# A graph network of four layers on one core: buffer order, division order and a transfer route changed together

## The chip, the cores and the metric

The kernel runs on one core of a Trainium2 chip. A core has TensorE (matrix products, PE in the profile; its loads of weights are PEld), VectorE (DVE), ScalarE (ACT), GpSimd (POOL) and SyncE (SP). SP, GpSimd and ScalarE also issue transfers (DMA), which sixteen DMA engines carry out. Each engine works through its own queue in order and waits on semaphores. The metric is the device time of one execution in microseconds (us); lower is better. Before the change the median of three runs is 3392.79 us (3391.16 to 3394.97).

## The reference

The input is a matrix `x` of 3327 nodes by 512 features and a sparse 0/1 adjacency `adj` of 3327 by 3327. Four layers follow each other, and each is `x = layernorm(x + layer(x, adj))`.

Layers 0, 2 and 3 are graph attention. For layer 3, cut to what matters:

```
h = (x @ W).reshape(N, 4, 128).transpose(1, 0, 2)        # a projection, 4 heads
e = leaky_relu(si[:, :, None] + sj[:, None, :], 0.2)     # si, sj: h times the two halves of a
e = where(adj > 0, e, -9e15)
h_prime = softmax(e, axis=-1) @ h                        # a sum over neighbours, per head
return elu(h_prime)                                      # heads side by side: N x 512
```

Layers 0 and 2 have eight heads of 64 features; layer 0 has no `elu`. Layer 1 takes the mean over the first 64 neighbours of each node, projects it and the node itself, and adds the two.

## The kernel before, in words

The nodes are cut into `NT` = 26 row tiles of 128. All intermediate tensors between the stages lie in DRAM: `hd` holds the sums of an attention over the neighbours before they are divided by the denominators, `rec` (on chip) the reciprocals of these denominators, and `x2`, `x3` the results of the layers, which are the residuals of the next.

**Attention** (`unit`, from line 364). An attention layer runs over two halves of the result's rows (13 tiles, 1664 nodes) and, within a half, over four slots `s`: two heads of 64 in layers 0 and 2, one head of 128 in layer 3. A unit is one (half, slot). Over the 26 tiles `j` of source nodes, VectorE makes the unnormalised weights `t` (line 405), ScalarE makes a mask `y` of the larger branch from them (line 408), and TensorE adds the products of `t` and the projected features `vj` into four PSUM banks `po` (line 428), and those of `y` into banks `pd` for the denominators (line 380). Three buffers of `t` let VectorE be ahead of TensorE. At the unit's end `po`, features by nodes, is copied to `ob` and has to be transposed. There are two ways:

- `by_dma`, in the first half of layer 3: VectorE transposes `po` in blocks of 32 by 32 into `ob` (line 446), and four transfers put the blocks at their places in `hd` (line 473).
- otherwise: VectorE copies the first bank (line 450) and ScalarE the other three (line 448), and during the following unit jobs of up to four TensorE transposes each (line 456) bring `ob` into `pt`. In layer 3's second half the function `final` takes `pt` from there: for heads 0 and 1 VectorE copies it into `g` (line 1010), a tile on chip with the second half's rows. The jobs `first_slots` later divide these columns of `g`, take the exponential and add the residual.

**The end of a layer** (`finish_steps`, lines 165 to 203). For `n` row tiles, `load` takes the sums `h` from `hd` and the residual `xr`; `divide` multiplies `h` by `rec` on VectorE (line 181) and, with `elu`, takes the exponential on ScalarE (line 186); `add` adds the residual (lines 194 and 195, or 197); `norm_rows` computes mean and variance (152, 153), the root (154), the reciprocal (155), a product (158) and scales on ScalarE (161). The tiles come from pools. A pool lays its tiles in memory in the order in which their names first appear, each with its number of buffers. A pool may lie over memory of pools closed before; its tile then waits for the last use of the older tiles that it lies over. So the order of names sets what a load waits for.

The function is used at the end of layers 0 and 2 for the first two tiles, in `sage` (layer 1, pool `sa`: six `h` of 2 KB, then two `xr`), in `third` (the last projection, pool `p_f`: ten `h`, six `xr`) and in layer 3's second half for the rows of the first.

In layer 1's first stage (963 to 1168 us) tile after tile is normalised, transposed (line 724) and multiplied with two matrices (732, 735). The tiles of layer 0's end that its loads lie over are those of layer 0's last unit. In the memory plan the six `h` of `sa` begin at byte 188672 of a partition and the two `xr` are at 200960 and 203008. Layer 0 used 182656 to 189311 for its last buffer of `t`, 189312 to 200959 for seven `y`, 200960 to 205055 for `vj`, and 200960 for the last small `hb`, which is stored to `hd`.

**The last projection** (`third`, from line 892). For every tile the result of layer 2 is finished, stored, transposed by TensorE (261), copied by ScalarE (262, `xT`), summed by VectorE (263, `xsum`) and, one tile later, multiplied with the weights (271); ScalarE takes three small parts of the product (`dc`, `rc`, `qc`, lines 272 and 275) and VectorE scales the rest (277, `vt`). Two tiles make a group. The loop's order in the text is:

```
for s, y in enumerate(ys):
    xT = L3.project1(pp, ps, y, t)            # transposes, xT, xsum
    if s == 0 and groups:
        ahead, steps = groups.pop(0)
        for f in steps:                       # divide, add, norm_rows of the next group
            f()
    if pend:
        L3.project2(pp, bank, wsb, *pend)
```

After tile 14 `prepare` and `cut` are called for the first half, small operations that make the next attention's columns.

**What sets the order.** TensorE's instructions stay as written. On the other engines and queues a planner picks, at each step, the earliest written instruction that its own estimate of times holds to be ready. An instruction whose data the planner believes to be there early may so stand in the queue far ahead of its place in the text; on the chip the engine waits for it all the same. `tc.keep_in_program_order(ins)` puts `ins` behind the instruction that was written just before it for the same engine. Before the change this holds for the exponential of tile 2 (`pinned` with `t0 == 2`, `s == 0`).

Of the kernel before, what the change touches and what calls it, by code (L numbers as in the profile page):

```python
# [7 lines left out]
F32 = mybir.dt.float32  # L8
# [5 lines left out]
ALU = mybir.AluOpType  # L14
# [4 lines left out]
P = 128  # L19
# [13 lines left out]
def kernel(  # L33
# [10 lines left out]
    nc = tc.nc  # L44
    N, F = x.shape
# [66 lines left out]
    rec = const.tile([P, NT, 8], F32, name="rec")  # L112
# [52 lines left out]
    def finish_steps(pool, xin, layer, t0, n, hbufs=6, eng=nc.sync, xbufs=None, xpool=None, ebufs=None, pinned=False):  # L165
        H, D = layer.H, layer.D
        ys, xs, steps = [], [], []

        def load():
            for t in range(t0, t0 + n):  # L170
                h = pool.tile([P, F], F32, name="h", bufs=hbufs)
                load_tile(h, hd, t, eng)
                ys.append(h)
                xr = xpool.tile([P, F], F32, name="xr", tag="hb") if xpool else \
                    pool.tile([P, F], F32, name="xr", bufs=xbufs)
                load_tile(xr, xin, t, nc.gpsimd)
                xs.append(xr)

        def divide(s):
            h = ys[s]  # L180
            nc.vector.tensor_tensor(h.rearrange("p (h d) -> p h d", h=H), h.rearrange("p (h d) -> p h d", h=H),
                                    rec[:, t0 + s, :H].rearrange("p (h e) -> p h e", e=1).to_broadcast([P, H, D]),
                                    op=ALU.mult)
            if layer.elu:
                e = pool.tile([P, F], F32, name="e", bufs=ebufs)
                ins = nc.scalar.activation(e, h, AF.Exp)
                if pinned and s == 0:
                    tc.keep_in_program_order(ins)
                xs.append(e)

        def add(s):
            h, xr = ys[s], xs[s]
            if layer.elu:
                nc.vector.scalar_tensor_tensor(xr, xs[n + s], 1.0, xr, op0=ALU.min, op1=ALU.add)
                nc.vector.scalar_tensor_tensor(h, h, 0.0, xr, op0=ALU.max, op1=ALU.add)
            else:
                nc.vector.tensor_tensor(h, h, xr, op=ALU.add)

        steps.append(load)
        for s in range(n):  # L200
            steps += [lambda s=s: divide(s), lambda s=s: add(s)]
        steps.append(lambda: norm_rows(pool, ys, t0))
        return ys, steps

    def finish(*a):
        ys, steps = finish_steps(*a)
        for f in steps:
            f()
        return ys
# [16 lines left out]
    class Layer:  # L226
# [137 lines left out]
        def unit(self, pools, half, s, background, aside, final=None, ending=None):  # L364
            H, D, HS = self.H, self.D, self.HS
# [73 lines left out]
            den(NT - 2, late)  # L439

            ob = sp.tile([P, IW], F32, name="ob", bufs=1)
            by_dma = HS == 1 and not final
            for c, (a_, z) in enumerate(CUTS):
                if by_dma:

# [5 lines left out]
            t0 = half * HALF  # L451
# [16 lines left out]

            nothing = lambda: None
            jobs = [nothing, nothing]  # L470
            if by_dma:
                for b in range(4):
                    nc.sync.dma_start(out=hd[i0:i0 + IW, s * P + 32 * b:s * P + 32 * b + 32]
                                      .rearrange("(q i) f -> i q f", i=32),
                                      in_=ob[32 * b:32 * b + 32, :].rearrange("p (q f) -> p q f", f=32))
# [16 lines left out]
            if not by_pe:  # L492
# [3 lines left out]
                for c in range(2):  # L496
                    ins = nc.vector.transpose(db[:64, c * (WA // 2):(c + 1) * (WA // 2)], pd[c][:64, :WA // 2])
# [394 lines left out]
    def third(first):  # L892
        with tc.tile_pool(name="col3", bufs=1) as cp, tc.tile_pool(name="at_r3", bufs=2, reuse_waits="tile") as rp:
# [3 lines left out]
            with tc.tile_pool(name="p_w", bufs=1, reuse_waits="tile") as wp, \  # L897
# [13 lines left out]
                def load_group(t0):  # L911
                    if t0 < NT:
                        groups.append(finish_steps(fp, x2, L2, t0, 2, 10, nc.gpsimd if t0 < 4 else nc.sync, 6,
                                                    pinned=t0 == 2))
                        groups[-1][1].pop(0)()

                load_group(2)
# [3 lines left out]
                for t0 in range(0, NT, 2):  # L921
# [4 lines left out]
                    for s, y in enumerate(ys):  # L926
# [3 lines left out]
                        if s == 0 and groups:  # L930
                            ahead, steps = groups.pop(0)
# [14 lines left out]
            with tc.tile_pool(name="f3", bufs=2) as fp, tc.tile_pool(name="f4", bufs=1) as gp:  # L946
                g = gp.tile([P, HALF, F], F32, name="g")
# [57 lines left out]
                    return [divide, add]  # L1005

                def final(s, q0, n, pt):
                    qs = slice(q0, q0 + n)
                    if s < 2:
                        nc.vector.tensor_copy(g[:, qs, s * P:(s + 1) * P], pt[:, :n])  # L1010
                        return

                    y = g[:, qs, s * P:(s + 1) * P]
                    held = {}
# [210 lines left out]
```

## Time and profile before

| | us |
|---|---|
| median of three runs | 3392.79 |
| the profiled execution | 3389.15 |
| its span, first to last instruction | 3387.4 |
| busy in the span: PE, PEld | 3251.2, 1626.4 |
| busy in the span: DVE, ACT, POOL | 2687.5, 2354.6, 239.8 |

| stage | from and to, us | PE busy | DVE busy | ACT busy |
|---|---|---|---|---|
| layer 0, attention | 137 to 958 | 796.66 | 806.43 | 753.93 |
| layer 1, first stage | 958 to 1168 | 194.15 | 137.79 | 71.06 |
| layer 1, second stage | 1168 to 1755 | 572.32 | 252.15 | 199.82 |
| layer 2, attention | 1755 to 2553 | 781.78 | 791.54 | 738.53 |
| last projection | 2553 to 2690 | 119.16 | 110.95 | 100.14 |
| layer 3, first half | 2690 to 3020 | 328.85 | 211.53 | 177.66 |
| layer 3, second half and end | 3020 to 3387 | 341.80 | 294.74 | 285.71 |

The profile shows one execution. A line of a timeline gives start and duration in us, the engine (PE, PEld, DVE, ACT, POOL; SPq for the issue of a transfer by SP), the line of the kernel, the operation, output and inputs, the count, and in brackets how long the engine had stood idle before and what it waited for. A line of the chain (the work that ended last, followed back from the end) gives start, duration, engine, output and line. Times of TensorE are modelled from its pipelining, so that a busy TensorE need not be at its peak.

### The profile page before, as it was taken

What the parts mean: (1) busy time and instruction counts of PE and PEld (TensorE: products, weight loads), DVE (VectorE), ACT (ScalarE), POOL (GpSimd) and SP (SyncE); (2) the same over time, 40 slices, a digit from 0 to 9 for tenths busy, and PEclk for the clock granted to TensorE, in tenths of its full rate; (3) what the DMA queues carried; (4) which work ended last, traced back from release to release, by engine and by line L of the source; (5) the groups of instructions that cost most, each with busy time, mean ns of one, the idle gap of its engine ahead of it and who ended that gap; (6) DMA issues with size and microseconds to landing.
All of it is one profiled execution on the core that took longest, in us unless ns stands there. A gap on an engine that the chain in (4) does not pass through costs nothing.

```text
span 3387.4 us, 47182 instructions
## 1 busy us (share of the span) xinstructions
PE 3251.2 (96%) x18476; PEld 1626.4 (48%) x18476; DVE 2687.5 (79%) x2619; ACT 2354.6 (70%) x2143; POOL 239.8 (7%) x389
## 2 busy tenths in 40 slices
PE   8899999999979999999989999999998999999997
PEld 7634344444434445545544444444446754455453
DVE  5799999999967544444449999999998766668887
ACT  2398998999953333333338999999997655558986
POOL 3100000000010011111110000000002000010110
PEclk9999999999999999999999999999998999999998
DMA  9644111110143343333320111111117411122211
GB/s 368 222 124 127 49 49 38 55 49 28 44 123 125 122 117 84 91 85 87 80 77 20 47 48 50 51 48 47 35 31 241 152 41 42 41 51 80 94 42 49
DMA packets 288014, 284.29 MB, mean 84 GB/s; under 512 B 107492, under 2 KB 223534, under 8 KB 287791
## 3 DMA queue, kind: packets, MB, share of 16 engines
q1 hardware_dynamic: 254063, 170.62, 16.6%
q0 software_dynamic: 28208, 102.96, 9.5%
q10 hardware_dynamic: 5520, 7.69, 0.7%
q8 instruction: 146, 2.39, 0.3%
q14 instruction: 77, 0.63, 0.1%
HBM read 212.01 MB, written 69.17 MB: 83 GB/s over the span
## 4 chain that ended last, share of the span: by engine, by line
PE 85%; DVE 5%; DMA 4%; ACT 3%; issue 2%; SPq 0%; ACTq 0%; DVEq 0%; POOL 0%; POOLq 0%
PE po L428 52%; PE acc L859 12%; PE pd L380 7%; PE pw L271 5%; DVE t L405 3%; PE pz L732 3%; DMA raw<-in_adjT_dram 3%; PE pi L735 3%; ACT y L408 1%; PE pt L456 1%; PE pk L819 1%; DMA h<-hd 0%; PE pa L1108 0%; PE pt L724 0%; PE pct L664 0%
## 5 line engine op out<-in xcount | busy, mean ns | idle before, releaser
L405 DVE SCALAR_TENSOR_TENSOR t<-rb,qc,mask 128x1664 f32<-128x1664 f32 x1040 | 1960.3, 1954 | 169.4 <-PE po L428 147.3
L408 ACT ACTIVATE y<-t,bi,sc 128x1664 fp8e4<-128x1664 f32 x1040 | 1769.5, 1766 | 310.4 <-PE pd L380 292.7
L428 PE MATMUL po<-t,vj 128*64 128x448 f32 (+3 forms) x8320 | 1909.6, 521 | 22.1 <-DVE t L405 19.6
L428 PEld LDWEIGHTS po<-t,vj 128*64 128x64 f32 (+1 forms) x8320 | 838.9, 148 | 970.6 <-issue 704.0
L859 PE MATMUL acc<-zs,kt 128*128 128x512 bf16 x1352 | 401.1, 380 | 0.0
L271 PE MATMUL pw<-wsb,xT 128*128 128x264 f32 (+1 forms) x1248 | 302.2, 397 | 15.2 <-DVE vt L277 12.0
L859 PEld LDWEIGHTS <-kt 128*128 128x128 fp8e4 x2002 | 196.1, 98 | 242.1 <-issue 7.7
L811 ACT CAST pk<-cy 128x512 f32<-128x512 bf16 x169 | 99.0, 588 | 277.4 <-DVE kt L823 266.3
L271 PEld LDWEIGHTS pw<-wsb,xT 128*128 128x128 f32 x1248 | 241.1, 197 | 60.7 <-ACT xT L262 10.8
L380 PE MATMUL pd<-y,sden 128*32 128x448 fp8e4 (+1 forms) x4160 | 259.5, 342 | 10.4 <-ACT y L408 10.4
L859 PE MATMUL acc<-zl,kt 128*128 128x512 bf16 x650 | 246.5, 379 | 0.0
L380 PEld LDWEIGHTS <-sden 128*32 128x32 bf16 x4160 | 117.5, 96 | 162.5 <-issue 139.8
L823 DVE SCALAR_TENSOR_TENSOR kt<-pk,mask 128x512 fp8e4<-128x512 f32 x169 | 116.1, 688 | 94.0 <-PE pk L819 94.0
L277 DVE TENSOR_TENSOR vt<-pw,dc 128x256 f32<-128x256 f32 x156 | 59.0, 418 | 148.2 <-ACT dc L272 143.7
L359 POOL DMA_DIRECT2D rb<-r x40 | 21.3, 532 | 1670.4 <-DVE t L405 1652.2
L275 ACT COPY rc<-pw 128x8 f32<-128x8 f32 (+1 forms) x78 | 12.6, 162 | 156.6 <-PE pw L271 154.1
L831 DVE SCALAR_TENSOR_TENSOR y<-acc,cnt,bnb 128x512 f32<-128x512 f32 x26 | 19.5, 751 | 97.7 <-PE acc L859 90.3
L732 PE MATMUL pz<-wn,xT 128*128 128x512 f32 x208 | 94.9, 600 | 1.7 <-ACT xT L726 1.7
L700 POOL DMA_DIRECT2D cy<-ctd x91 | 67.9, 746 | 385.1 <-ACT pk L811 312.6
L735 PE MATMUL pi<-wl,xT 128*128 128x512 f32 x208 | 93.5, 592 | 0.0
L634 DVE TENSOR_SCALAR mask<-raw 128x832 fp8e4<-128x832 int32 (+2 forms) x90 | 54.8, 614 | 38.9 <-DMA raw<-in_adjT_dram 38.5
L154 ACT ACT_TABLE_LOAD x45 | 57.7, 1283 | 37.0 <-DVE mv L153 36.4
(187 smaller groups left out, 1699.3 us busy)
## 6 DMA issues: line engine op xcount, KB each, us to landing
vj<-v SPq DMA_DIRECT2D x312, 128.0 KB
rb<-r POOLq DMA_DIRECT2D x40, 832.0 KB, 4.8
raw<-in_adjT_dram SPq DMA_DIRECT2D x67, 416.0 KB
cy<-ctd POOLq DMA_DIRECT2D x78, 256.0 KB, 4.0
h<-hd SPq DMA_DIRECT2D x61, 256.0 KB
v<-vt SPq DMA_DIRECT2D x50, 256.0 KB
hd<-hb SPq DMA_DIRECT2D x48, 256.0 KB
xr<-x POOLq DMA_DIRECT2D x45, 256.0 KB, 3.1
```

The costliest lines, as they stand in the source:

```text
L271: nc.tensor.matmul(pw[e][:, :FW + H], xT[:, c, :], wsb[:, c, e, :], start=c == 0, stop=c == FC - 1)
L277: nc.vector.tensor_tensor(vt[:, hs, :], pw[e][:, :FW].rearrange("p (h d) -> p h d", d=D), self.dc[:, t, hs].rearrange("p (h e) -> p h e", e=1)
L380: nc.tensor.matmul(pd[c][32 * kk:32 * kk + 32, :w_], lhsT, rhs, start=(kk, c) not in seen, skip_group_check=final is not None, stop=last a ...
L405: nc.vector.scalar_tensor_tensor(t, rb[k], self.qc[:, j, h:h + 1], mask[:, j, i0:i0 + IW], op0=ALU.max, op1=ALU.mult)
L408: nc.scalar.activation(y, t, AF.Sigmoid, bias=self.bi[:, j, h:h + 1], scale=self.sc[:, j, h:h + 1], saturate=False)
L428: nc.tensor.matmul(po[c][k * D:(k + 1) * D, :z - a_], vj[:, j % 2, k * D:(k + 1) * D], ts[k][:, a_:z], start=j == 0, stop=j == NT - 1)
L700: nc.gpsimd.dma_start(out=cy[:, :n, :], in_=ctd[t:t + n, b * GW:(b + 1) * GW] .rearrange("(o t) i -> o t i", o=1).to_broadcast([P, n, GW]))
L732: nc.tensor.matmul(pz, xT[:, c, :], wn[:, c, :], start=c == 0, stop=c == FC - 1)
L735: nc.tensor.matmul(pi, xT[:, c, :], wl[:, c, :], start=c == 0, stop=c == FC - 1)
L811: nc.scalar.copy(pks[k % 2], carry[b, t // 4 * 4][:, t % 4:t % 4 + 2, :])
L823: nc.vector.scalar_tensor_tensor(kt, pk, NEIGHBOURS, mask[:, t:t + 2, i0:i0 + GW], op0=ALU.is_le, op1=ALU.mult, saturate=False)
L859: nc.tensor.matmul(acc, kts[t][:, s * P:(s + 1) * P], zs(t, c) if c < 2 else zl[:, t, :], start=t == 0 and c == 0, stop=t == NT - 1 and c ...
```

## The change

It has three parts.

1. In `finish_steps`, `load` asks for the tile `xr` before the tile `h`. The transfers keep their order. In a pool in which neither name has appeared before, the buffers of `xr` now come first.
2. In `third`, every group is `pinned`. For such a group both divisions are written before both additions, and from tile 4 on (`t0 > 2`) each division stays behind the VectorE instruction written before it: for the first of a group that is `xsum` of the first tile of the group before. The exponential of tile 2 is kept in order as before.
3. In the second half of layer 3, heads 0 and 1 take the route `by_dma`. VectorE transposes in blocks into `ob`, and sixteen transfers per head, issued on SP, bring the blocks from `ob` to their places in `g`, both on chip. The TensorE transposes and the copies by VectorE and ScalarE of these two heads are gone.

```diff
         def load():
             for t in range(t0, t0 + n):
+                xr = xpool.tile([P, F], F32, name="xr", tag="hb") if xpool else \
+                    pool.tile([P, F], F32, name="xr", bufs=xbufs)
                 h = pool.tile([P, F], F32, name="h", bufs=hbufs)
                 load_tile(h, hd, t, eng)
                 ys.append(h)
-                xr = xpool.tile([P, F], F32, name="xr", tag="hb") if xpool else \
-                    pool.tile([P, F], F32, name="xr", bufs=xbufs)
                 load_tile(xr, xin, t, nc.gpsimd)
...
         def divide(s):
             h = ys[s]
-            nc.vector.tensor_tensor(h.rearrange("p (h d) -> p h d", h=H), h.rearrange("p (h d) -> p h d", h=H),
+            ins = nc.vector.tensor_tensor(h.rearrange("p (h d) -> p h d", h=H), h.rearrange("p (h d) -> p h d", h=H),
...
+            if pinned and t0 > 2:
+                tc.keep_in_program_order(ins)
             if layer.elu:
                 e = pool.tile([P, F], F32, name="e", bufs=ebufs)
                 ins = nc.scalar.activation(e, h, AF.Exp)
-                if pinned and s == 0:
+                if pinned and (t0, s) == (2, 0):
                     tc.keep_in_program_order(ins)
...
         steps.append(load)
-        for s in range(n):
-            steps += [lambda s=s: divide(s), lambda s=s: add(s)]
+        if pinned:
+            steps += [lambda s=s: divide(s) for s in range(n)] + [lambda s=s: add(s) for s in range(n)]
+        else:
+            for s in range(n):
+                steps += [lambda s=s: divide(s), lambda s=s: add(s)]
...
-            by_dma = HS == 1 and not final
+            by_dma = HS == 1 and (not final or s < 2)
...
-            if by_dma:
+            if by_dma and final:
+                for b in range(4):
+                    for m in range(4):
+                        final(s, b, m, ob[32 * b:32 * b + 32, :].rearrange("p (q m f) -> p q m f", m=4, f=32)[:, :, m, :])
+            elif by_dma:
...
-                                                    pinned=t0 == 2))
+                                                    pinned=True))
...
                 def final(s, q0, n, pt):
+                    if s < 2:
+
+                        nc.sync.dma_start(out=g[32 * n:32 * n + 32, :, s * P + 32 * q0:s * P + 32 * q0 + 32], in_=pt)
+                        return
                     qs = slice(q0, q0 + n)
-                    if s < 2:
-                        nc.vector.tensor_copy(g[:, qs, s * P:(s + 1) * P], pt[:, :n])
-                        return
```

More of the change, by code (lines that the diff above doesn't have):

```diff
@@ L180, in divide @@
             h = ys[s]
-            nc.vector.tensor_tensor(h.rearrange("p (h d) -> p h d", h=H), h.rearrange("p (h d) -> p h d", h=H),
-                                    rec[:, t0 + s, :H].rearrange("p (h e) -> p h e", e=1).to_broadcast([P, H, D]),
-                                    op=ALU.mult)
+            ins = nc.vector.tensor_tensor(h.rearrange("p (h d) -> p h d", h=H), h.rearrange("p (h d) -> p h d", h=H),
+                                          rec[:, t0 + s, :H].rearrange("p (h e) -> p h e", e=1).to_broadcast([P, H, D]),
+                                          op=ALU.mult)
+            if pinned and t0 > 2:
+                tc.keep_in_program_order(ins)
             if layer.elu:
```

## The prediction

> **What bounds the kernel now.** I read the page first: TensorE is busy for 96% of the span and its lines hold 85% of the chain that ended last. So a stretch where TensorE is fed gains only what TensorE itself is spared, and the rest lies in its holes. I then went through the chain, the timeline of each engine and a table of stretches for the three places which the edits touch.
>
> Place 1, layer 0 to layer 1. In the timelines of GpSimd, VectorE and TensorE:
>
> ```profile
> 969.73 0.54 POOL L126 DMA_DIRECT2D xr<-in_x_dram  x1 [9.92 <-issue]
> ...
> 967.63 0.69 DVE L181 TENSOR_TENSOR h<-h,rec 128x512 f32<-128x512 f32 x1 [5.85 <-DMA h<-hd]
> 972.85 0.69 DVE L197 TENSOR_TENSOR h<-h,xr 128x512 f32<-128x512 f32 x1 [4.53 <-DMA xr<-in_x_dram]
> 977.21 0.69 DVE L181 TENSOR_TENSOR h<-h,rec 128x512 f32<-128x512 f32 x1 [2.25 <-DMA h<-hd]
> ...
> 983.97 1.11 PE L724 MATMUL pt<-ident,h 128*128 128x128 f32 x4 [13.84 <-ACT h L161]
> ```
>
> GpSimd stands for 9.92 us before it loads the residual of row tile 2; VectorE waits for that residual, and TensorE idles 13.84 us for the normalised tile. The memory plan says on what GpSimd waits: that buffer lies at byte 200960, over the last `hb` of layer 0, whose store leaves last.
>
> Place 2, the last projection, in the timelines of VectorE and TensorE and the table of stretches (us and count for PE, PEld, DVE, ACT, POOL, then clock, DMA share and GB/s):
>
> ```profile
> 2562.96 1.40 DVE L181 TENSOR_TENSOR h<-h,rec 128x512 f32<-128x512 f32 x2 [4.52 <-DMA h<-hd]
> ...
> 2573.51 1.12 PE L261 MATMUL pt<-ident,h 128*128 128x128 f32 x4 [8.46 <-ACT h L161]
> ...
> 2600.00:2620.00 20.00, 17.72 (x90) 15.05 (x89) 19.19 (x45) 13.80 (x36) 1.61 (x3) 1.00 0.75 251
> 2660.00:2680.00 20.00, 20.00 (x103) 17.37 (x103) 8.85 (x17) 8.68 (x25) 0.00 (x0) 1.00 0.25 96
> ```
>
> VectorE is stuck 4.52 us in a division for tile 4, whose sums are late, while the additions of tile 2, ready since the exponentials ended at 2560.62, queue behind it; TensorE idles 8.46 us. Later VectorE works far ahead (19.19 of 20) and ends early (8.85 of 20).
>
> Place 3, the last layer's second half. The chain at the start of head 1, then the one place that shows the new route, the end of the first half:
>
> ```profile
> 3115.28 0.44 PE pt L456 x4
> 3115.71 2.80 PE po L428 x8
> 3118.51 0.49 PE pd L380 x6
> ...
> 3018.86 2.10 DVE L446 STREAM_TRANSPOSE ob<-po 128x448 f32<-128x448 f32 x4
> ...
> 3020.99 4.46 SPq L473 DMA_DIRECT2D hd<-ob  x4
> ```
>
> TensorE's transposes of the previous head stand on the path, and the transposing by VectorE with four stores went by there without a hole.
>
> **What the Trainium skill says.** Perfetto Trace Analysis, Tensor Engine Instruction, calls VectorE and ScalarE strict FIFOs: the 4.52 us above are such a queue. ScalarE: Activation LUTs, What ACT_TABLE_LOAD costs, gives 1283 ns for a load plus 1380 ns of drain; the loads here last 1283 ns, but a root follows a load by 0.01 us (2585.83, 2587.12), so only 1.28 is priced. TensorE: Matmul & The Clock Gate, What's actually happening, lets the clock fall after about 3.4 us of idleness: after 8.46 us sixteen products took 5.42 instead of 3.67 us, after 1.30 us they took 3.75; the trace agrees. DMA: Bandwidth & Descriptors, Why small descriptors are slow, exempts transfers within SBUF; nothing before shows one of that kind.
>
> **Part 1: residual buffers first.** No instruction changes. In layer 1's pool two `xr` (4 KB) move ahead of six `h`, so tile 2's and 3's residuals land at 188672 and 190720, over `t` and `y`, which are free when the last `pd` products end at 958.28. GpSimd then issues the four loads of tiles 2 and 3 from 959.26 in a row, 0.54 each, to 961.4. The 0.75 MB more that now move share the engines with 0.96 MB of stores at some 340 GB/s, so they land by 970.4 (estimate). Then the add 0.7, statistics and aggregate 0.85, root 0.35, reciprocal and product 0.4, the first scaling 0.8 and handovers 0.15: the transposes start at 973.65 instead of 983.97, **-10.3**. From there TensorE is full (40.00 of 40 in three stretches from 1000), so it reaches the end. Late next is the load of `h` for tile 4, which now lies over that `hb` and stands behind six small loads on SP (landed 977.2): TensorE needs tile 4 at about 988. It costs nothing unless VectorE's queue again has tile 4's division ahead of tile 3's addition; then nearly all of the gain is gone (bounds -12 and -1). The other pools: in the last projection the two waits (1.20 and 1.09 us on GpSimd) only change hands, between `xr` and `h`; in the last layer `xr` had its place already. Zero, bounded by 1 us either way.
>
> **Part 2: divisions in written order.** Each group's first division from tile 4 on is queued behind `xsum` of the group before; no work comes or goes. First the gain: tile 2's additions follow the exponentials at once: four at 0.6 to 0.7 (2559.7 to 2562.3), statistics 1.4, one `xsum` 0.6, root, reciprocal and product 0.9, scaling 0.8: 2566.0 instead of 2573.51, **-7.5**.
>
> Then the loss: groups can no longer run ahead. One period, scaling to scaling: two scalings 1.5, copy of `xT` 0.59, `xsum` 0.60, first division 0.68, exponential 0.63, four additions 2.5, statistics 1.28, aggregate 0.17, root 0.29, reciprocal 0.16, product 0.16, and nine handovers of 0.05: 9.0 us. TensorE needs 7.9 for two tiles (0.44 + 3.51 each), so the chain bounds. VectorE has 2.1 us of other work per group (four `vt` at 0.37, one `xsum` at 0.6); I put half inside the chain: 10.1. The halves of `prepare` and `cut`, 5.4 us of VectorE once, find 2 us free per period: 3 us remain. Tiles 2 to 24 are eleven groups: 11 x 10.1 + 3 = 114.1 us; before, 2672.70 - 2573.51 = 99.2. **+14.9**. Bounds for the period: 9.0 with all else in gaps (99.0, so -0.2), 11.4 with a table load of 1.28 in every chain (128.4, so +29.2).
>
> **Part 3: two heads by transfer.** Removed: 26 transposes, in the chain 0.44 x 3 + 0.11 for head 0 and 0.59, 0.58, 0.59, 0.11 for head 1: 3.3 us of TensorE. ScalarE loses three copies a head (1.5 us), VectorE trades one copy (0.62) and four (2.34) for four transposes (2.1 to 2.3). SP gets 2 x 16 issues; 416 pieces of 128 bytes each are 6656 a head, as many as the four stores of one head before (4.46 us of issue; DMA busy until about 3029). Queued behind them on SP: `vj`, three pairs ahead (19 us), and a load of `h`, for which VectorE already waited 2.83 us at 3107.83. I charge 0.8 us for that and for VectorE's 1.7 us more at the turn into head 2. **-2.5**; bounds -3.5 and +3.
>
> **Sum.** -10.3 - 7.5 + 14.9 - 2.5 = -5.4 us on the profiled 3389.15 (span 3387.4 and 1.75 around it): 3383.7. The median of the runs is 3392.79, 3.64 higher, so 3387.4.
>
> **Rivals.** *Short chain*: the planner puts VectorE's other work into gaps, period 9.3, 1.5 for `prepare`: 103.8, so +4.6; sum -15.7, 3377. For it: VectorE loses its 6.1 us of waits for `h`, and has 2 us idle in each period. Against: a filler between reciprocal and product is common now (2587.45 to 2588.71).
> *Long chain, slower*: in the last projection each root is followed by an exponential set's load for `dc` before the scaling, as now at 2613.43 and 2631.26: period 11.4, 128.4 us, sum +8.9, 3402. The whole comes out at zero from a period of 10.6, and slower from 11.2.
> *Place 1 keeps its hole*, because tile 4's division blocks as at 977.21: gain 1 instead of 10.3, 3396.7. The change then does not do there what it says.
>
> **How the numbers follow.** Sum 0.35 (3382 to 3392 alone), short chain 0.30, long chain 0.18, hole kept 0.17. About 0.2%, 6.8 us, can be told from no change: 3386.0 to 3399.6. Faster: 0.14 of the first and nearly all of the second, 0.42. Same: 0.21, 0.015, 0.02 and 0.14, 0.39. Slower: 0.19. The range takes the second and third cases in: 3372 to 3404.
>
> **What would show it.** Right: GpSimd's residual load near 960, TensorE's hole at 970 down to 4 us; no wait of L181 for DMA near 2560; the transposes of L261 in pairs every 10 us with 1 to 2 us idle; L456 26 fewer, no new hole near 3107 and 3191. Wrong: the hole at 970 above 10 us; a period at 9 or 11.4; VectorE waiting for `h` behind the sixteen transfers, which would empty TensorE after 3107.

## The result, and the profile after

The changed kernel takes 3424.31 us (median of 4 runs, 3419.2 to 3425.14) beside 3392.23 us for the kernel before in the same session: a ratio of 1.0096, 95% interval 1.0084 to 1.0108. It is 32 us slower, where 5 us less was forecast. Its profiled execution spans 3423.0 us, 35.6 more than before.

Stage by stage, from TensorE's timeline of each profiled execution. "Sage" runs from the last `po` product of layer 0 to the last `acc` product, "layer 2" on to its last `po`, "projection" on to the last `pw`, "heads" on to TensorE's last instruction. "Start" is the part of the projection up to tile 2's transposes; "pair" is the mean time from one even tile's transposes to the next over the eleven groups from tile 2 to tile 24. All in us.

| kernel | sage | layer 2 | projection | start | pair | heads |
|---|---|---|---|---|---|---|
| before | 791.0 | 804.6 | 140.1 | 25.5 | 9.0 | 677.1 |
| after | 796.1 | 806.4 | 162.1 | 21.1 | 11.4 | 683.1 |

The differences are 5.1, 1.8, 22.0 and 6.0 us, 34.9 together. Not all of it can be read: in the eleven profiled executions below that leave part 1 out, the sage stage took 790.5 to 793.7 us, so that "before" lies at the low end of the scatter.

**Place 1.** Timelines of GpSimd, VectorE and TensorE of the changed kernel:

```profile
959.76 0.54 POOL L126 DMA_DIRECT2D xr<-in_x_dram  x1
...
967.92 0.69 DVE L199 TENSOR_TENSOR h<-h,xr 128x512 f32<-128x512 f32 x1 [1.13 <-DMA xr<-in_x_dram]
978.34 0.69 DVE L181 TENSOR_TENSOR h<-h,rec 128x512 f32<-128x512 f32 x1 [8.32 <-issue]
978.95 0.68 DVE L199 TENSOR_TENSOR h<-h,xr 128x512 f32<-128x512 f32 x1
...
985.05 1.12 PE L733 MATMUL pt<-ident,h 128*128 128x128 f32 x4 [14.36 <-ACT h L161]
```

The residual load is issued 10 us earlier and tile 2's addition runs 5 us earlier. Then VectorE stands 8.32 us at tile 4's division, with tile 3's addition behind it, and TensorE's hole is as long as before: 14.36 beside 13.84 us. The profile names no releaser for the 8.32 us; the transfer of tile 4's `h` was issued on SP at 975.32, where it was 972.89 before, and the same kind of wait is marked with it in a run below.

**Place 2.** TensorE's timeline, the table of the same two stretches, and a piece of the chain of waits:

```profile
2576.03 1.12 PE L266 MATMUL pt<-ident,h 128*128 128x128 f32 x4 [3.17 <-ACT h L161]
...
2646.96 1.12 PE L266 MATMUL pt<-ident,h 128*128 128x128 f32 x4 [4.46 <-ACT h L161]
...
2701.38 0.66 PE L266 MATMUL pt<-ident,h 128*128 128x128 f32 x4 [2.05 <-ACT h L161]
```

```profile
2600.00:2620.00 20.00, 16.01 (x73) 13.08 (x71) 16.39 (x41) 12.07 (x28) 2.15 (x4) 0.93 0.70 230
2660.00:2680.00 20.00, 16.13 (x71) 13.08 (x70) 15.73 (x36) 12.49 (x25) 2.15 (x4) 0.91 0.48 184
```

```profile
2678.51 0.29 ACT rs L154
2678.82 1.28 ACT L277
2680.11 0.17 ACT dc L277
2680.28 1.41 ACT h L161 x2
```

The wait of a division for late sums is gone and the start is 4.4 us shorter. But VectorE no longer works ahead (16.39 and 15.73 us busy where it was 19.19 and 8.85), TensorE idles 1 to 4.5 us for the scaled tile in eleven of the twelve even tiles, and in the second stretch it does 71 products and transposes where it did 103. (2701.38 - 2576.03) / 11 = 11.4 us a group. The chain now holds a root, the table load for `dc` and the scaling in a row.

**Place 3.** Timelines of SP, VectorE, GpSimd and TensorE at the start of head 2, then TensorE at the turn into head 3 and the chain ahead of that:

```profile
3219.70 11.34 SPq L1019 DMA_DIRECT2D g<-ob  x16
3231.14 0.56 SPq L516 DMA_DIRECT2D dd<-red  x1
...
3222.69 0.94 DVE L514 TENSOR_REDUCE red<-db 128x112 f32<-128x336 f32 x2
...
3233.63 9.33 POOL L526 DMA_DIRECT2D pes<-dd  x16 [9.68 <-DMA dd<-red]
...
3226.20 7.55 PE L433 MATMUL po<-t,vj 128*128 128x448 f32 x16 [2.09 <-DVE t L410]
3308.32 0.54 PE L385 MATMUL pd<-y,sden 128*32 128x448 fp8e4 x6 [4.47 <-ACT y L413]
```

```profile
3303.47 1.28 ACT L1006
3304.76 0.42 ACT e L1006
3305.20 1.28 ACT L413
3306.49 1.78 ACT y L413
```

The way of the partial sums, in the kernel before (VectorE and SP) and, last, after:

```profile
3198.16 0.96 DVE L505 TENSOR_REDUCE red<-db 128x112 f32<-128x336 f32 x2
3199.41 0.46 SPq L507 DMA_DIRECT2D dd<-red  x1
3214.90 0.25 DVE L530 TENSOR_TENSOR pes<-pes 128x104 f32<-128x104 f32 x1
...
3255.32 0.26 DVE L539 TENSOR_TENSOR pes<-pes 128x104 f32<-128x104 f32 x1
```

At the start of head 2 TensorE waits 2.09 us for `t`, which VectorE makes only after the transposes of `ob` (from 3217.56) and `db` and the reduction. The partial sums are reduced at 3223.6, but their store stands behind sixteen issues until 3231.14. The sums are finished at 3255.32, 32.6 us after the reduction began, where it took 16.7 before. The divisions and exponentials that need them slide to the end of the head, and each exponential costs two table loads among the `y`s (at L1006 and L413 above): TensorE waits 4.47 us where before there was no wait. Of the 2.09 us not all is new: at the turn into head 2 TensorE waited 1.78 us before, and 0.96 and then 2.09 after.

### The profile page after: what moved, and what is told of

It reads as the page before. It is cut to its first block, busy times and chain, and to the rows that moved or that the text cites. A ratio compares the mean times of both kernels' runs of the same rounds, so it can differ in the third digit from the quotient of the medians.

```text
span 3423.0 us, 47189 instructions
## 1 busy us (share of the span) xinstructions
PE 3264.8 (95%) x18450; PEld 1631.4 (48%) x18450; DVE 2686.1 (78%) x2617; ACT 2363.7 (69%) x2143; POOL 240.2 (7%) x389
## 4 chain that ended last, share of the span: by engine, by line
PE 79%; DVE 7%; issue 7%; DMA 4%; ACT 3%; POOL 0%; SPq 0%; DVEq 0%; POOLq 0%; ACTq 0%
PE po L433 48%; PE acc L868 12%; PE pd L385 7%; PE pw L276 5%; DVE t L410 4%; DMA raw<-in_adjT_dram 2%; PE pz L741 1%; PE pi L744 1%; ACT y L413 1%; PE pk L828 1%; PE pt L461 1%; DMA asb<-in_a_dram 1%; PE pa L1118 0%; DMA h<-hd 0%; PE pt L266 0%
## 5 line engine op out<-in xcount | busy, mean ns | idle before, releaser
L413 ACT ACTIVATE y<-t,bi,sc 128x1664 fp8e4<-128x1664 f32 x1040 | 1769.4, 1766 | 317.1 <-PE pd L385 292.1
L276 PE MATMUL pw<-wsb,xT 128*128 128x264 f32 (+1 forms) x1248 | 308.8, 403 | 15.0 <-DVE vt L282 12.7
L868 PEld LDWEIGHTS <-kt 128*128 128x128 fp8e4 x2002 | 196.9, 98 | 244.9 <-issue 12.1
L280 ACT COPY rc<-pw 128x8 f32<-128x8 f32 (+1 forms) x78 | 12.6, 162 | 166.4 <-PE pw L276 163.8
```

The source lines that it names most:

```text
L276: nc.tensor.matmul(pw[e][:, :FW + H], xT[:, c, :], wsb[:, c, e, :], start=c == 0, stop=c == FC - 1)
L413: nc.scalar.activation(y, t, AF.Sigmoid, bias=self.bi[:, j, h:h + 1], scale=self.sc[:, j, h:h + 1], saturate=False)
L868: nc.tensor.matmul(acc, kts[t][:, s * P:(s + 1) * P], zs(t, c) if c < 2 else zl[:, t, :], start=t == 0 and c == 0, stop=t == NT - 1 and c ...
```

## The experiments

Each ratio is against runs of the kernel before on the same chip (medians of 3389.65 to 3391.67 us), with its 95% interval. Stage times are measured as above. The diffs of the three single parts are against the kernel before; the others show how the lines of the change, or lines that it left alone, were edited.

### One part at a time

Part 1 alone:

```diff
+                xr = xpool.tile(...) if xpool else pool.tile([P, F], F32, name="xr", bufs=xbufs)
                 h = pool.tile([P, F], F32, name="h", bufs=hbufs)
...
-                xr = xpool.tile(...) if xpool else pool.tile([P, F], F32, name="xr", bufs=xbufs)
```

> Part 1 alone on the kernel before. Theory 1 (the hole between layer 0 and layer 1 stays because tile 4's division blocks VectorE in front of tile 3's addition, and the second stage of the sage layer loses some 5 us by another order of its loads): TensorE restarts at about 985 as in the changed kernel, the last product into acc comes some 5 us later than before (1748 instead of 1743), the time is 3397 to 3400. Rival (the 5 us in that stage have nothing to do with part 1): the acc products end at 1743 to 1744 and the time is 3392 to 3394.

3392.96 us, 1.0007 (0.9999 to 1.0016). TensorE restarted at 986.58 after 15.02 us of idleness, and tile 4's division stood 8.20 us in front of tile 3's addition: the hole is there with part 1 alone, as theory 1 has it. The time is the rival's, and can't be told from no change. The sage stage took 796.5 us, above the scatter, but this profile is of the slowest of the kernel's executions (3397.56 us), and three kernels below with part 1 and another order took 792.3, 793.5 and 795.0. So the stage's loss is not settled: it lies at the edge of what one profile tells.

Part 2 alone:

```diff
+            if pinned and t0 > 2:
+                tc.keep_in_program_order(ins)
...
+        if pinned:
+            steps += [lambda s=s: divide(s) for s in range(n)] + [lambda s=s: add(s) for s in range(n)]
...
-                                                    pinned=t0 == 2))
+                                                    pinned=True))
```

> Part 2 alone. Theory 2 (written order forces each group's whole chain, with a table load in it, between two groups): the transposes of the last projection come every 11.4 us per pair of tiles instead of 9.0, its first transposes after the wait come 4 to 7 us earlier, and the kernel is 19 to 24 us slower, 3411 to 3417. Rival (the period of 11.4 needs part 1's memory plan too, since residuals and sums lie elsewhere in the last projection): period 9.0 to 10.1, time 3386 to 3400.

3409.52 us, 1.0053 (1.0038 to 1.0068). Start 20.6, pair 11.4, projection 162.1: all of the projection's 22 us. The time lies 1.5 us below the range that was expected.

Part 3 alone:

```diff
-            by_dma = HS == 1 and not final
+            by_dma = HS == 1 and (not final or s < 2)
...
+                        nc.sync.dma_start(out=g[32 * n:32 * n + 32, :, s * P + 32 * q0:s * P + 32 * q0 + 32], in_=pt)
```

> Part 3 alone. Theory 3 (sixteen issues on SP hold back the store of the partial sums, so the reciprocals of heads 0 and 1 and the exponentials behind them come some 12 us late in head 2, and TensorE idles 4 us at the turn into head 3): 4 to 8 us slower, 3396 to 3400, with the loss between the starts of head 2 and of the tail. Rival (that loss comes of part 2's later table loads or of a shifted clock): no loss, -2.5 us as priced, 3390.

3396.19 us, 1.0018 (1.0012 to 1.0025). TensorE shows the same two waits as in the changed kernel, 2.09 and 4.47 us; the heads took 682.0. The turn from head 0 to head 1 has no wait. Against 3390.12 us before, the three parts alone add to 2.8 + 19.4 + 6.1 = 28.3 us, beside the 32.1 of the whole.

The written order without the holding:

```diff
-            if pinned and t0 > 2:
-                tc.keep_in_program_order(ins)
```

> Of part 2 only the order in which a group's steps are written (both divisions, then both additions), nothing held in place. If the holding is what costs (theory 2): the planner places the divisions ahead as before, period 9.0, time within 3 us of before, 3390 to 3396. If the written order itself costs (rival): period above 10, time above 3403.

3389.88 us, 0.9998 (0.9990 to 1.0007), projection 140.2. Without the holding the planner puts the divisions ahead again, and nothing changes: the holding is the costly part.

### Place 1: what stands in front of the second addition

First hold, with part 1 alone: tiles 4 and 5 queued behind tile 3's addition.

```diff
+            with tc.issue_after(held_add[0].ins) if layer.li == 0 and t0 == 4 else ExitStack():
+                divide1(s)
...
+                ins = nc.vector.tensor_tensor(h, h, xr, op=ALU.add)
+                if layer.li == 0 and t0 == 2:
+                    held_add[:] = [ins]
```

> Part 1 alone, and the two divisions of tiles 4 and 5 of layer 0 queued behind tile 3's addition on VectorE (an order, no wait). Theory 1: tile 3's addition no longer stands behind a division whose sums are late, so TensorE restarts 10 us sooner, at 974 to 977 with a hole of 4 to 6 us, and 7 to 10 us of it reach the end: 3380 to 3384. Rival (something else is late next, or the gain is lost again in the later stage, which TensorE doesn't fill there): restart at 980 or later, or time above 3388.

3390.98 us, 1.0006 (0.9998 to 1.0015). VectorE's timeline:

```profile
973.69 0.68 DVE L203 TENSOR_TENSOR h<-h,xr 128x512 f32<-128x512 f32 x1
978.66 0.69 DVE L187 TENSOR_TENSOR h<-h,rec 128x512 f32<-128x512 f32 x1 [4.29 <-issue]
979.27 0.69 DVE L154 BATCH_NORM_STATS2 st<-h 128x6 f32<-128x512 f32 x1
```

The addition ran 5 us earlier; the division now stood in front of the statistics, and the hole was 14.23 us. The time is the rival's.

Second hold: tiles 4 and 5 behind the last step of the statistics, and ScalarE's cast of the counts, which had waited for its load until 972 in front of the copies of `zs`, in written order.

```diff
+            with tc.issue_after(held_norm[-1].ins) if layer.li == 0 and t0 == 4 else ExitStack():
...
-                        nc.scalar.copy(cf, cr)
+                        tc.keep_in_program_order(nc.scalar.copy(cf, cr))
```

> Part 1 alone, with the divisions of tiles 4 and 5 of layer 0 queued behind the last step of the statistics of tiles 2 and 3 (not only behind tile 3's addition), and ScalarE's cast of the neighbour counts, which waits for its own load until 972, queued in written order, so that it no longer stands in front of the copies of zs. Theory 1 (the residuals do come early, and what keeps the hole is the queue in front of the second addition and the statistics): TensorE restarts at 973 to 976 instead of 984 to 985, hole 3 to 6 us, time 3380 to 3384. Rival (the gain is real there but the rest of the stage gives it back, since its loads are late as well): restart as said, but the last product into acc at 1742 to 1745 as before and the time within 3 us of before.

3395.16 us, 1.0007 (1.0001 to 1.0014). VectorE's timeline again:

```profile
972.99 0.16 DVE L157 RECIPROCAL rs<-rs 128x2 f32<-128x2 f32 x1
982.09 0.69 DVE L187 TENSOR_TENSOR h<-h,rec 128x512 f32<-128x512 f32 x1 [8.94 <-DMA h<-hd]
982.70 0.15 DVE L160 SCALAR_TENSOR_TENSOR rs<-mv,rs 128x2 f32<-128x2 f32 x1
```

Now it is tile 6's division, not held, that stands 8.94 us in front of the very last step. The hole was 14.84 us.

Third: all of layer 0's divisions from tile 4 on.

```diff
-            with tc.issue_after(held_norm[-1].ins) if layer.li == 0 and t0 == 4 else ExitStack():
+            with tc.issue_after(held_norm[layer.li].ins) if layer.li == 0 and t0 > 2 else ExitStack():
```

> Part 1 alone, with all divisions of layer 0 from tile 4 on queued behind the statistics of tiles 2 and 3, and the cast of the counts in written order. In the run before with two held divisions the next one free, tile 6's, stood for 8.94 us in front of the last step of the statistics. Theory 1: with none left to step in, TensorE restarts at 972 to 975 as the prediction had it (hole 3 to 5 us); of the 10 us gained 7 or more reach the end, 3380 to 3384. Rival (given back in the stage behind): restart as said, acc's last product less than 3 us earlier than before, time within 3 us of before.

3386.71 us, 0.9988 (0.9981 to 0.9994). VectorE and TensorE:

```profile
976.75 0.16 DVE L160 SCALAR_TENSOR_TENSOR rs<-mv,rs 128x2 f32<-128x2 f32 x1
980.07 1.37 DVE L189 TENSOR_TENSOR h<-h,rec 128x512 f32<-128x512 f32 x2 [3.16 <-DMA h<-hd]
...
977.82 1.12 PE L735 MATMUL pt<-ident,h 128*128 128x128 f32 x4 [6.01 <-ACT h L165]
```

The division waits where nothing urgent stands behind it, the hole is 6.01 us, and the sage stage took 785.5, below all scatter. From the end of layer 0's products to the restart it is 23.7 us, beside 31.5 before and 21.2 in the prediction. No run has this hold without part 1, and it also orders ScalarE's cast, so what of the gain is part 1's own is not shown. The median is 4.2 us below that of before (3390.90), less than the 7 expected.

### Place 2: what makes 11.4 us

All on part 2 alone unless it is said. First the exponential of `dc`, replaced by a constant (so the column's exponential is left out):

```diff
-            nc.scalar.activation(self.dc[:, t, :], pw[1][:, FW:FW + H], AF.Exp, scale=ALPHA)
+            if self.li == 3:
+                nc.scalar.activation(self.dc[:, t, :], pw[1][:, FW:FW + H], AF.Identity, bias=one, scale=0.0)
```

> Part 2 alone, with the exponential of dc in the last layer's projection replaced by a constant (scale 0, bias 1: the column's exponential is left out), so that no table load stands between a root and the scaling. Theory 2a (the load of 1.28 us in the chain is what makes 11.4 out of 10.1): period 10.0 to 10.3, the projection 12 to 15 us shorter than with part 2 alone, time 3394 to 3398. Theory 2b (the load only moves in front of the exponential of e, which is in the chain as well): period 11.2 or more, time 3406 to 3410.

3417.98 us, 1.0080 (1.0060 to 1.0100), pair (2701.62 - 2568.72) / 11 = 12.1. ScalarE's timeline:

```profile
2678.47 1.28 ACT L190 ACT_TABLE_LOAD   x1 [1.40 <-DVE h L183]
2679.77 1.15 ACT L190 ACTIVATE e<-h 128x512 f32<-128x512 f32 x2
...
2683.45 0.16 ACT L285 COPY rc<-pw 128x4 f32<-128x4 f32 x1 [1.78 <-PE pw L278]
...
2684.23 1.28 ACT L156 ACT_TABLE_LOAD   x1
2685.52 0.30 ACT L156 ACTIVATE rs<-mv,eps 128x2 f32<-128x2 f32 x1
```

The load moved in front of `e`, where it began only once the division was there, so it lies in the chain again, and the root stands behind the copies of TensorE's products. The period is that of theory 2b; the kernel became 8 us slower than with part 2 alone, more than either theory had.

Then those copies, held back behind the next scaling:

```diff
+            with tc.issue_after(scaled[-1].ins) if self.li == 3 and t % 2 == 0 and 2 < t < NT - 2 else ExitStack():
+                nc.scalar.activation(self.dc[:, t, :], pw[1][:, FW:FW + H], AF.Exp, scale=ALPHA)
```

(and the same around the copies to `rc` and `qc`)

> Part 2 alone, with ScalarE's three copies and exponentials from the second tile's products (rc, dc, qc of even tiles from 4 on) queued behind the scaling of the next group, so that the root no longer queues behind TensorE's last product. Theory 2c (in the slow groups the root stands behind those copies on ScalarE, so TensorE's own 9 us, slowed by its idling, lie in the loop, and a table load after them): period 9.5 to 10.3, projection 11 to 20 us shorter than with part 2 alone, 3390 to 3399. Rival (the loop is VectorE's chain of divisions, additions and statistics with a table load, as priced): period 11 or more, 3406 to 3412.

3421.88 us, 1.0089 (1.0074 to 1.0104), pair (2705.63 - 2569.89) / 11 = 12.3. VectorE's timeline:

```profile
2684.97 0.76 DVE L286 TENSOR_TENSOR vt<-pw,dc 128x256 f32<-128x256 f32 x2 [3.13 <-ACT rc L284]
2685.64 0.68 DVE L270 TENSOR_REDUCE xsum<-xT 128x4 f32<-128x512 f32 x1
2686.23 1.28 DVE L183 TENSOR_TENSOR h<-h,rec 128x512 f32<-128x512 f32 x2
```

The root was freed, but now `vt` waits 3.13 us for the late `dc`, and `xsum` and the held divisions are queued behind `vt`. One group, around `prepare`, took 22.69 us, since a copy held back there kept TensorE waiting for `rc`; the other ten took 11.3 on the mean, beside 11.2 for ten of part 2 alone without its longest. So the period stayed, and the further loss is mostly the hold's own. In this run and the one before, the wait moved to another place: neither takes one cause away alone.

Then all loads taken away: the root is left out for tiles 4 to 25 (the variance itself is inverted), with part 2 and, as a control, on the kernel before.

```diff
-        nc.scalar.activation(rs[:, :n, 0], mv[:, :n, 1], AF.Sqrt, bias=eps)
+        nc.scalar.activation(rs[:, :n, 0], mv[:, :n, 1], AF.Sqrt if root else AF.Identity, bias=eps)
...
-        steps.append(lambda: norm_rows(pool, ys, t0))
+        steps.append(lambda: norm_rows(pool, ys, t0, not (pinned and t0 > 2)))
```

> Part 2 alone, with the square root of the variance left out for tiles 4 to 25 of the last projection (the variance itself is inverted), so that ScalarE needs no table load there at all. Theory 2d (one load of 1.28 us lies in every loop, wherever the planner puts it, and the rest is VectorE's chain): period 9.2 to 10.2, projection 13 to 22 us shorter than with part 2 alone, time 3388 to 3397. Rival (the loop is long because copies and vt queue ahead of the division and the root; loads only fill waits): period above 10.8, time above 3403.

> The kernel before with the same roots left out, as the control. If the loads are hidden there by the lead of VectorE: projection within 2 us of before, 3388 to 3394. If they bound it too: 5 us or more faster.

With part 2: 3393.16 us, 1.0007 (0.9998 to 1.0015), projection 141.8, 20.2 less than with the roots. On the kernel before: 3382.44 us, 0.9971 (0.9959 to 0.9983), projection 131.9, 8.2 less. TensorE's timeline with part 2 and no roots:

```profile
2599.64 0.66 PE L266 MATMUL pt<-ident,h 128*128 128x128 f32 x4 [1.54 <-ACT h L161]
...
2609.29 0.66 PE L266 MATMUL pt<-ident,h 128*128 128x128 f32 x4 [1.54 <-ACT h L161]
...
2618.94 0.66 PE L266 MATMUL pt<-ident,h 128*128 128x128 f32 x4 [1.54 <-ACT h L161]
```

A regular 9.65 us. The Trainium skill (ScalarE: Activation LUTs, Table sets: the hidden batching unit) has the identity in every set; the trace agrees, with no load among these groups. So of part 2's 22.0 us in the projection, 12.0 (20.2 - 8.2) go with the loads and what they bring with them, and 10.0 (141.84 - 131.88) stay without any load. What they bring is more than their 1.28 us each. With no load in the way the planner also put the root's instruction in front of the copies of TensorE's products, and TensorE hardly slowed. The stretch from tile 2 to tile 24, first with part 2 alone, then without roots (columns as in the table above):

```profile
2567.67:2693.56 125.89, 100.16 (x453) 82.46 (x454) 90.93 (x225) 82.90 (x171) 9.90 (x19) 0.92 0.54 178
2569.47:2677.39 107.92, 92.32 (x454) 76.63 (x454) 90.93 (x227) 55.72 (x151) 9.90 (x19) 0.98 0.64 215
```

TensorE's same products kept it busy 7.8 us longer at a mean granted clock of 0.92 instead of 0.98. How much of the 12.0 belongs to the loads' own time, to the order and to the clock, no run separates. The control's own expectation, that the loads are hidden before, was wrong: TensorE is then full there (20.00 of 20 us from 2600), so the roots had cost the kernel before 8 us too, 5.1 of them in the one group around `prepare` (14.84 us before, 9.74 without).

The distance of the hold: each division behind `xsum` of the group before the last.

```diff
-            if pinned and t0 > 2:
-                tc.keep_in_program_order(ins)
+            with tc.issue_after(behind[0].ins) if pinned and t0 > 2 and behind else ExitStack():
```

> Part 2 with each division held behind xsum of the group before the last instead of the last, so that it may run one group further ahead. Theory 2 (the period is long because a group's chain can't overlap the one before it): period back to 9.0 to 9.3, the start's gain of 4 to 7 us kept, time 3383 to 3388. Rival (the period comes of the table loads or of VectorE's work, whatever the distance): period above 10, time above 3400.

3395.58 us, 1.0017 (1.0010 to 1.0023), pair 9.65, projection 146.2: one more group of lead takes 16 of the 22 us back with all roots in place. That is less than theory 2 expected (period 9.0 to 9.3, at most 3388). The start was 24.5; its gain was lost, since tile 4's divisions could again pass tile 2's additions.

Only tiles 4 and 5 held as the change holds them:

```diff
-            if pinned and t0 > 2:
+            if pinned and t0 == 4:
```

> Part 2 with only the two divisions of tiles 4 and 5 held in written order (the order of writing as in the change for all groups). Theory 2: the start gains 4 to 5 us, since nothing stands in front of tile 2's additions, and the later groups run ahead as before with a period of 9.0: 3384 to 3388. Rival (the start's gain is used up, since VectorE then bounds the middle of the projection anyway): within 2 us of before.

3395.06 us, 1.0012 (1.0006 to 1.0019), start 24.9, projection 144.7. VectorE's timeline:

```profile
2568.84 1.34 DVE L181 TENSOR_TENSOR h<-h,rec 128x512 f32<-128x512 f32 x2 [5.70 <-DMA h<-hd]
2570.09 1.28 DVE L196 SCALAR_TENSOR_TENSOR xr<-e,xr 128x512 f32<-128x512 f32 x2
```

Two divisions still stand 5.70 us in front of tile 2's additions: in VectorE's order they are those of tiles 6 and 7. The next group has stepped in, as at place 1.

All divisions from tile 4 on behind tile 2's and 3's statistics, free after that, on the kernel before:

```diff
+            with tc.issue_after(held_norm[layer.li].ins) if pinned and t0 > 2 else ExitStack():
```

> The kernel before, with the divisions of tiles 4 and later in the last projection queued behind the statistics of tiles 2 and 3 alone and free after that. Theory 2: the start's gain of 4 to 7 us without the longer period: transposes of tile 2 at 18 to 21 us after the attention's end instead of 25.5, period 9.0 to 9.2, 3383 to 3388. Rival (VectorE, pressed by the work that it could not do ahead, gives it back by the middle): within 2 us of before.

3389.17 us, 0.9996 (0.9987 to 1.0005). The start is 20.5, 5.0 better, and the groups after it take 3.1 more: the first 12.7 instead of 10.1, the one around `prepare` 17.3 instead of 14.8. The time is the rival's. Its reason, that VectorE could not work ahead at the start, fits the long first group, but no run tests it.

### Place 3: the store of the sums

```diff
-                nc.sync.dma_start(out=dd, in_=red.rearrange("p b o s -> p b (o s)"))
+                (nc.gpsimd if final else nc.sync).dma_start(out=dd, in_=red.rearrange("p b o s -> p b (o s)"))
```

> Part 3 alone, with the store of the partial sums of the last layer's second half issued on GpSimd instead of SP, so that it doesn't stand behind the sixteen transfers. Theory 3 (that delay costs the loss): the sums come back 7 us sooner, the wait of 4.47 us at the turn into head 3 goes or falls below 1 us, time 3389 to 3392. Rival (the loss is VectorE's order at the start of head 2, 2.09 us, and slower products after it): the time stays at 3395 to 3397.

3389.00 us, 0.9998 (0.9989 to 1.0006), beside 1.0018 with the store on SP. SP, GpSimd and VectorE:

```profile
3192.15 11.07 SPq L1017 DMA_DIRECT2D g<-ob  x16
3196.37 0.57 POOL L514 DMA_DIRECT2D dd<-red  x1 [5.24 <-DVE red L512]
3198.87 9.36 POOL L524 DMA_DIRECT2D pes<-dd  x16 [1.70 <-DMA dd<-red]
...
3212.74 0.26 DVE L537 TENSOR_TENSOR pes<-pes 128x104 f32<-128x104 f32 x1
```

From the reduction (3195.13) to the finished sums it is 17.6 us, beside 30.9 with part 3 alone and 16.7 before. The wait at the turn into head 3 is down to 0.24 us, the 2.08 us at the start of head 2 stays. The heads took 675.5; kernels without part 3 took 675.4 to 678.6, so the repaired part 3 costs and gains nothing that can be told.

### Joined

Part 1 with the second hold, the hold of tiles 4 and 5 in the projection and the repaired part 3:

> All that seems to gain, together: part 1 with both holds of the run before, the divisions of tiles 4 and 5 alone held in the last projection, part 3 with the store of the partial sums on GpSimd. If the three add up: -7 for the first, -4 for the second, -1 for the third, 3376 to 3381. If a gain of the first two is lost before the end: 3384 to 3390.

3402.93 us, 1.0037 (1.0024 to 1.0050). Two of the three were no repairs, as the two sections above show; the projection took 149.0.

Part 1 with the third hold and the free start, without and with the repaired part 3:

> Part 1 with all late divisions of layer 0 held (as e_hold3) and the start of the last projection held (as e_start), without part 3. If the two gains add: -4.2 and -1.7, 3384 to 3386. If the second is only noise or is lost: 3386 to 3388.

> The same with part 3, the store of the partial sums on GpSimd. Part 3 then should cost nothing or gain up to 1 us: 3383 to 3386. If its waits at the start of head 2 cost more with these other orders: 3387 or more.

Without: 3385.36 us, 0.9985 (0.9979 to 0.9992). With: 3384.33 us, 0.9982 (0.9975 to 0.9988), 5.8 us below before (3390.09) and the fastest kernel here that computes all. The pair's difference of 1.0 us lies within the two intervals. Nor can either be told from part 1 with the third hold alone (0.9988, 0.9981 to 0.9994), so what the free start adds is not shown.

## Why the prediction was wrong, step by step

**Place 1, -10.3: wrong by the condition it named.** "It costs nothing unless VectorE's queue again has tile 4's division ahead of tile 3's addition" was the step, and it does. The residuals' early load (959.76) was right. With every division held and the cast in order, the restart gained 7.8 us, so the size was near. The term that was too small is VectorE's path to the scaling: it puts the five steps of tile 0's output (L749 to L757 there) among the additions and statistics, the last three from 974.54 to 976.56, and the reciprocal came 1.9 us after the last aggregate, where a root of 0.35 us was counted.

**Place 2, start: -7.5, measured -4.4** (-4.9 with part 2 alone). The division's wait was gone and the additions began when forecast (11.6 us after the attention). The mis-sized term is the tail: a `vt` that waits 2.11 us for `dc` (1.55 with part 2 alone), and a root behind that `dc`, on which the reciprocal waits another 0.84.

**Place 2, the period: the step that failed is "I put half inside the chain: 10.1".** That sum prices the steps of VectorE and ScalarE; it has no table load in it, no products of TensorE in front of a root and no slower clock. Without loads the loop measured 9.65, so the steps that it has were sized well. With the roots it took 11.4 on the mean, 1.6 us more than the same run of part 2 without them ((125.89 - 107.92) / 11).

The eleven groups after the change are not of one kind. In six the load of `dc` stands between root and scaling, as the rival "long chain" had it: three of these took 10.2 us, the others 10.8, 11.4 and 11.9, and in these three the first tile's sixteen products took 5.4 to 6.1 instead of 3.67 us. In four the root and its own load stand behind copies of TensorE's products, so that TensorE's time lies in the loop as well: 11.3 (three) and 14.25. In that longest one TensorE's granted clock fell to 0.5 (2619 to 2626) and sixteen products took 6.22 us. The last, 12.6, has `prepare`, with loads on both sides of the root.

So the rival had the number 11.4 but only half of the mechanism: where its load came alone and the products ran in 3.67 us, the period was 10.2. That this is near 10.1 is luck, since 10.1 had no load and half of VectorE's other work in its place. The 3 us for `prepare` and `cut` are not shown: one group stands 1.2 us above the mean, and without roots it took 9.80 beside 9.65. By how much each, the order and the clock, lengthens the loop stays open.

**Place 3, -2.5: the step that failed is "Queued behind them on SP: `vj` ... and a load of `h`".** The list left out `dd<-red`, which is traced after the sixteen transfers; measured +6.1. What the list did name cost nothing at the turn into head 1. Of the marks, "no new hole near 3107" was right, and "3191" wrong: TensorE waited 0.96 and 2.09 us there for the 1.78 before. The Trainium skill (ScalarE: Activation LUTs, What ACT_TABLE_LOAD costs) prices every switch to a different set; here a delay of 16 us in the sums was enough to crowd exponentials with two switches of 1.28 us each into the end of a head.

**The sum.** On the profiled executions' own times, 3383.7 us forecast and 3424.8 measured, 41.1 us are to be explained: 14.6 more in the projection (+22.0 for +7.4), 8.5 more in the heads (+6.0 for -2.5) and 10.3 not gained. That leaves 7.7, of which the sage stage's +5.1 and layer 2's +1.8; the scatter of single profiles covers a part of them, and the rest is not settled. The cases had been weighed as if one at a time could come true. "Hole kept" and "long chain" rest on different engines' queues in different stages, and both came true together with the unseen wait; no case and no end of the range held such a sum.

## What to carry to other kernels

When a load is made earlier, look at who stands in front of its user in the user's queue: holding back one late instruction lets the next late one in, and only a hold on all of them moved TensorE. An order that forbids one engine to run a group ahead can bring the table loads, copies and handovers of the other engines into the period, and the idleness that follows can slow TensorE besides. When issues are added to a queue, list every instruction traced behind them, the small stores first, and put the one with a chain behind it on another queue.

## What the runs showed of the hardware that was not expected

- A table load in front of an exponential that waits began only after the wait (2678.47, 1.40 us idle, then 1.28), while the load in front of a root began at once and was over before the root could start (part 2 alone: load at 2678.46, root at 2680.86 after 1.12 us more of waiting).
- Sixteen transfers within SBUF of 52 KB each (416 pieces of 128 bytes) hold SP for 10.6 to 12.1 us, 0.7 us each, where four stores of the same bytes in all to DRAM took 4.46.
- TensorE could be slow after less idleness than the 3.4 us that the prediction cites, and fast after as much: with part 2 alone sixteen `pw` took 5.36 us after 2.05 and after 2.34 us of it, 3.67 after 2.07, and after 3.17 us once 4.62 and once 3.67. The granted clock was 0.50 among slow ones (2663 to 2666) and 1.00 among fast ones (2613.87 to 2617.54). The length of the last idleness alone does not tell which; here the measurements decide.
- The same instructions in the sage stage differ by 3 us from one profiled execution to the next, so a loss of that size is not read from one pair of profiles.
